# New state of a gated graph layer: turned by VectorE in two pieces instead of by TensorE, with x loaded in short runs and layer 1's rows fetched back from DRAM

## The chip, the cores and the metric

The kernel runs on one core of a Trainium2 chip. The core has TensorE (matmuls, written to PSUM), VectorE (DVE in the profile), ScalarE (ACT), GpSimd (POOL) and SyncE (SP, which here only issues DMAs). GpSimd and SyncE each issue DMAs on a queue of their own, and 16 DMA engines move the data of both. Every engine takes its instructions in the order in which the program gives them. The metric is the device time of one execution in microseconds.

## What is computed

Two residual layers on x (128 graphs, 128 nodes, 256 channels, float32) with an adjacency matrix per graph. Layer 0 normalizes x, applies ReLU, and puts the result h through a convolution branch, a message branch and a gated update; layer 1 works on the first 25 nodes of each graph only.

```python
h = jnp.maximum(_layernorm(x, axis=-1), 0.0)
x = x + _L0_gnn_ref(h, adj, ...)      # layer 0, all 128 nodes
h = jnp.maximum(_layernorm(x, axis=-1), 0.0)
x = x + _L1_gnn_ref(h, adj, ...)      # layer 1: five groups of the first 25 nodes

def _L0_gnn_ref(x, ...):              # x is h here; d = 256
    ...                               # x_conv, x_nmp: the two branches
    x_in = jnp.concatenate([x_conv, x_nmp], axis=-1)
    gi = x_in @ w_ih.T + b_ih
    gh = x @ w_hh.T + b_hh
    ...                               # cut into thirds: r, z, n
    r = jax.nn.sigmoid(gi_r + gh_r)
    z = jax.nn.sigmoid(gi_z + gh_z)
    nn_ = jnp.tanh(gi_n + r * gh_n)
    return (1.0 - z) * nn_ + z * x
```

## The kernel before

The 128 graphs are worked in 32 groups of four (q = 0 to 31). A group's state is kept with channels on the partitions: the tile `hT` is [128 channels, 2 halves of the 256 channels, 512 tokens], the 512 tokens being 4 graphs of 128 nodes. x in DRAM, and the output, have tokens as rows of 256 channels (1 KB), so the new state has to be turned before it is added to x.

There are three stretches. Up to about 690 us the kernel normalizes x, runs the convolution in the frequency domain (`stage_a`, `stage_b`) and, beside it, starts the message branch (`early`). From there to about 1947 us `stage_c(q)` does the gates of one group after the other, with the rest of the message branch and most of layer 1 between its steps. After that only layer 1 is left, which works on blocks of 16 graphs (blocks 0 to 7; block k needs the groups 4k to 4k+3).

The order of all engines' instructions is written by a small planner (`Lane`, `Order`): each piece of work is a generator that yields its cost in TensorE time and a delay before its next step; the planner picks the lane with the least weighted work whose next step is due. A step that waits for a condition polls it every 0.5 us of planned time. So a delay in a `yield` is planned time: it sets where the following instructions stand in each engine's queue, not when they run. Real waits are by semaphore.

One `stage_c(q)`, in the order of its lines:

- L768 to L802: the matmuls of the first gates. ScalarE copies the first product to `u2` (L769); VectorE forms sums of the convolution branch (`tc`, helper at L586). The two early parts (L775) and the three small products (L788, L790) follow, with VectorE's L791 and L792; then L794 with ScalarE's sigmoid into `r`, L797 to L800 with VectorE's L798 (adds a product to `u2`) and L784 (the helper `gate`), then L802.
- L806: the inverse transform of the next group's convolution branch, with block transposes by VectorE (L705, from PSUM).
- L808: wait, in the plan, until group q - 1 has finished its end (`C_DONE`).
- L810 to L831: `z`. L817 and L818 allocate `xt` and load the group's x into it, with four DMAs on SyncE's queue.
- L834 to L862: the candidate state in `r`.
- L863 to L872: for each half of the channels ScalarE takes tanh into `r`, and GpSimd computes (h - n) * z + n with three operations of 128x512: L867, L868, L870. The last writes `z` with its columns permuted. After that the group counts as gated (`G_DONE`), and the next `stage_c` may start.
- L874 to L898, 11 us of planned time later, while the next group is running: TensorE transposes `z` in eight 128x128 pieces (L887) into two PSUM tiles `po`. VectorE adds the x of `xt`: the first 32 nodes of each graph go to the tile `X1` for layer 1 (L890), the other 96 stay in `xt` (L891, L893). GpSimd's queue stores those 96 nodes in four DMAs (L896), whose pieces are single rows of 1 KB. Then `C_DONE`.

Tiles without a `bufs` of their own exist once in this pool: `xt`, `z`, `r` and `u2` among them. `hTc` exists three times, `xm` and `xc` twice. Matmul results of the gates rotate through three PSUM banks (`pgat`), all others through five (`ptmp`).

`rows(q)` waits for `C_DONE` and normalizes the rows of `X1`: VectorE L945 to L947, GpSimd's power (L948), and 4 us of planned time later VectorE L951 and ScalarE L952. `block(blk)` multiplies (L1032, L1049, L1058 ...) and adds the result to `X1` (L1104), which GpSimd's queue stores (L1107). `prepare(blk)` makes layer 1's matrices: GpSimd adds (L970) that VectorE reduces at once (L975), and a chain over L995 to L998.

SyncE's queue carries, in one order, the loads of `hTc` and `xm` (L681, L683, for two groups ahead), of `yt` (L605), of `xt` (L381), of W1 (L935) and of small adjacency pieces (L964).

## Time and profile before

| | |
|---|---|
| median of 3 runs | 2039.76 us (2026.0 to 2566.76) |
| the profiled execution | 2034.12 us |
| its span, first to last instruction | 2032.3 us |
| granted TensorE clock, mean | 0.994 |
| L887, TensorE transposes of z | x256, 273 ns median |
| L890, L891, L893, VectorE adds of x | x32 each, 410, 416 and 681 ns median |
| L705, VectorE block transpose 128x512 from PSUM | x64, 710 ns median |
| L867, L868, L870, GpSimd gate operations 128x512 | x64 each, 1385, 1314 and 1310 ns mean |
| L896, GpSimd's issue of a store of 96 KB | x128, 552 ns median, 3.7 us from issue to landing |
| q0, the DMA queue that GpSimd issues on | 32656 packets, 93.98 MB, 14.2% of 16 engines' span |
| q1, the DMA queue that SyncE issues on | 157062 packets, 185.46 MB, 31.5% |

PE in the profile's lines is TensorE's matmuls, PEld its weight loads, which overlap them. A line of the timeline gives the start in us, the busy time in us, engine, source line, operation, what is written from what, and how many instructions were merged; in brackets stands the idle time of the engine before it and what ended that. A line of the busy times by stretch gives the stretch, its length, then each engine's busy time with its number of instructions, the granted TensorE clock, the DMA engines' busy share and GB/s. In the page's fifth part the groups of instructions carry count, total busy time and mean ns of one.

### The profile page before, as it was taken

Reading aid. Unit: us, or ns where it says so; the run is one execution under the profiler, and the core shown is the slowest. Engines: PE = TensorE matmul, PEld = TensorE weight load, DVE = VectorE, ACT = ScalarE, POOL = GpSimd, SP = SyncE. Lnnn points to the kernel's source line nnn. Section 1 sums busy time; section 2 is a strip of 40 time slices with the busy share of each in tenths; the row PEclk is TensorE's granted clock in tenths of the full one; section 3 lists DMA queues with packets and bytes.
Section 4 is the critical chain, followed back from the end, with each engine's and each line's share of the span. In section 5 each row is a group of like instructions: output and inputs, shape, how many; then the busy total and the mean of one; then the engine's idle time right before and its main releaser. Section 6 shows DMA issues by size and latency. Waiting matters only on the chain.

```text
span 2032.3 us, 34053 instructions
## 1 busy us (share of the span) xinstructions
PE 1989.3 (98%) x12852; PEld 1653.7 (81%) x12852; DVE 1285.2 (63%) x2807; ACT 683.8 (34%) x1547; POOL 741.2 (36%) x898
## 2 busy tenths in 40 slices
PE   7998999999999999999999999999999999999998
PEld 5666888889888888778788878878888888878875
DVE  6774445785433566766775775677577757766643
ACT  4663222454222344232322322232233322232233
POOL 3542666332655022532333233224323323332330
PEclk9999999999999999999999999999999999999999
DMA  9987879744877633432322322322232323232121
GB/s 214 297 266 226 269 255 285 222 145 161 269 257 254 188 115 89 147 90 68 105 73 84 96 83 73 97 83 80 82 108 68 90 84 93 79 100 84 37 82 53
DMA packets 190266, 281.91 MB, mean 139 GB/s; under 512 B 23745, under 2 KB 143494, under 8 KB 190102
## 3 DMA queue, kind: packets, MB, share of 16 engines
q1 hardware_dynamic: 157062, 185.46, 31.5%
q0 software_dynamic: 32656, 93.98, 14.2%
q8 instruction: 102, 1.67, 0.4%
q14 instruction: 62, 0.51, 0.1%
q10 hardware_dynamic: 384, 0.28, 0.1%
HBM read 187.34 MB, written 92.27 MB: 138 GB/s over the span
## 4 chain that ended last, share of the span: by engine, by line
PE 90%; DVE 3%; issue 2%; DMA 2%; POOL 2%; ACT 1%; SPq 0%; POOLq 0%; DVEq 0%; ACTq 0%
PE p L741 41%; PE pa L526 7%; PE pm L630 5%; PE ph L1049 5%; PE pz L1058 5%; PE pc L421 4%; PE pb L526 3%; PE px L656 3%; PE pf L432 3%; PE pi L698 3%; PE po L887 1%; PE ph L410 1%; PE py L1032 1%; PE pw L474 1%; PE pse L614 1%
## 5 line engine op out<-in xcount | busy, mean ns | idle before, releaser
L867 POOL TENSOR_TENSOR hTc<-hTc,r 128x512 f32<-128x512 f32 x64 | 88.7, 1385 | 255.8 <-ACT r L864 255.8
L526 PE MATMUL pa<-wf,X 128*128 128x256 f32 x640 | 152.2, 381 | 0.0
L558 DVE SCALAR_TENSOR_TENSOR y<-pa,kk 128x512 f32<-128x512 f32 x78 | 53.8, 690 | 151.2 <-ACT kk L557 151.1
L896 POOL DMA_DIRECT2D out<-xt x128 | 72.0, 569 | 175.1 <-DVE xt L893 172.0
L741 PE MATMUL p<-th,wrz 128*128 128x256 f32 x512 | 134.6, 385 | 0.0
L741 PE MATMUL p<-tc,wrz 128*128 128x256 f32 x512 | 131.5, 379 | 0.0
L741 PE MATMUL p<-tm,wrz 128*128 128x256 f32 x512 | 131.4, 379 | 0.0
L526 PEld LDWEIGHTS pa<-wf,X 128*128 128x128 f32 x640 | 118.2, 190 | 16.1 <-issue 2.0
L421 PE MATMUL pc<-c1w,hTa 128*128 128x256 f32 x512 | 122.3, 386 | 1.9 <-DVE X L438 1.7
L630 PE MATMUL pm<-wmsg,hT 128*128 128x256 f32 x512 | 123.4, 387 | 0.0
L1051 ACT ACTIVATE hh<-ph,vec 128x96 f32<-128x96 f32 (+3 forms) x160 | 63.8, 401 | 140.8 <-PE ph L1049 131.7
L1049 PE MATMUL ph<-yz,w 128*128 128x96 f32 (+3 forms) x640 | 109.7, 325 | 1.0 <-issue 1.0
L421 PEld LDWEIGHTS pc<-c1w,hTa 128*128 128x128 f32 x512 | 95.0, 192 | 18.9 <-DVE h L424 4.8
L741 PEld LDWEIGHTS p<-th,wrz 128*128 128x128 f32 x512 | 94.6, 190 | 19.1 <-issue 7.4
L630 PEld LDWEIGHTS pm<-wmsg,hT 128*128 128x128 f32 x512 | 97.0, 193 | 16.1 <-issue 1.6
L710 ACT ACTIVATE xc<-xc,t_bn 128x256 f32<-128x256 f32 x128 | 58.0, 500 | 149.2 <-DVE xc L707 149.2
L741 PEld LDWEIGHTS p<-tm,wrz 128*128 128x128 f32 x512 | 97.4, 190 | 13.1
L1058 PE MATMUL pz<-hh,w 128*128 128x96 f32 (+3 forms) x640 | 107.3, 322 | 0.0
L1049 PEld LDWEIGHTS ph<-yz,w 128*128 128x128 f32 x640 | 88.4, 194 | 21.3 <-issue 14.5
L741 PEld LDWEIGHTS p<-tc,wrz 128*128 128x128 f32 x512 | 95.0, 190 | 11.6
L1058 PEld LDWEIGHTS pz<-hh,w 128*128 128x128 f32 x640 | 86.6, 191 | 17.7
L741 PE MATMUL p<-hTc,wrz 128*128 128x256 f32 x384 | 98.9, 380 | 0.0
(200 smaller groups left out, 4579.5 us busy)
## 6 DMA issues: line engine op xcount, KB each, us to landing
wf<-wfd SPq DMA_DIRECT2D x160, 256.0 KB
wfd<-ws POOLq DMA_DIRECT2D x64, 320.0 KB, 9.2
yd<-y POOLq DMA_DIRECT2D x80, 256.0 KB, 4.1
yt<-yd SPq DMA_DIRECT2D x64, 320.0 KB
w<-in_W SPq DMA_DIRECT2D x40, 512.0 KB
xa<-in_x SPq DMA_DIRECT2D x128, 128.0 KB
hTd<-hTa POOLq DMA_DIRECT2D x32, 512.0 KB, 6.5
hT<-hTd SPq DMA_DIRECT2D x32, 512.0 KB
```

The source lines that it names most:

```text
L421: nc.tensor.matmul(pc[:, i], hT[:, k, (2 * h + i) * N:(2 * h + i + 1) * N], c1w[:, k], start=(k == 0), stop=(k == 1))
L432: nc.tensor.matmul(pf[:, i, :F * NB], h1[:, 2 * h + i, k * P:(k + 1) * P], fwd, start=True, stop=True)
L526: nc.tensor.matmul(ps, xk(k), WF[f][:, k, s], start=(k == 0), stop=(k == 1))
L630: nc.tensor.matmul(pm[:, i], hT[:, k, j * N:(j + 1) * N], LATE["wmsg"][:, k], start=(k == 0), stop=(k == 1))
L656: nc.tensor.matmul(px[:, dc, i], msgs[h][:, i, dc * P:(dc + 1) * P], aT[:, 2 * h + i], start=True, stop=True)
L698: nc.tensor.matmul(pi[w * WIDE:(w + 1) * WIDE, :, :, n].rearrange("p k g c -> p g k c"), inv[:F, o:o + WIDE], yt[:, n // 2::2].rearrange(" ...
L741: nc.tensor.matmul(ps[:, m], w[:, i, k, m * P:(m + 1) * P], factor(i, x, t), start=first and j == 0, stop=last and j == len(n) - 1, skip_g ...
L867: nc.gpsimd.tensor_sub(d, d, r[:, dc])
L896: nc.gpsimd.dma_start(out=out[q * GB + j, WIDE:].rearrange("(t n) c -> n t c", n=WIDE), in_=xt[j * WIDE:(j + 1) * WIDE, 1:4])
L1049: nc.tensor.matmul(ph, w1[:, k, m * P:(m + 1) * P], yz[:, k, :, o:o + n], start=(k == 0), stop=(k == 1))
L1051: nc.scalar.activation(hh[:, m], ph, AF.Relu, bias=v("b1", g * 4 + m))
L1058: nc.tensor.matmul(pz, w2[:, g, m, cc * P:(cc + 1) * P], hs[g][:, m], start=(m == 0), stop=(m == 3))
```

## The change

The new state is turned by VectorE, in blocks of 32x32, one half of the channels at a time, inside the following group's `stage_c`; the turned halves are written into `hT`, which is not needed any more. For this x is loaded into `xt` in a matching layout: partition 32a + s holds the tokens 16s to 16s + 15, and of each token the channels 32a to 32a + 31 of both halves. Its pieces in DRAM are 32 channels, 128 bytes. One add of 128x1024 then makes x1 for all 128 nodes. It is stored in the same layout to a DRAM tile `x1d`, and from there SyncE's queue fetches the first 32 nodes into `X1` and moves the other 96 to the output, DRAM to DRAM. Loads of x and stores to `x1d` are issued on GpSimd's queue, four DMAs each with 1024 pieces. The last gate operation writes `z` unpermuted. The plan no longer holds `stage_c(q)` until group q - 1 has finished its end; a lane `fetch` takes over `C_DONE`, 12 us of planned time after the store was issued (6 for the last group), plus 5 us for the fetch.

```diff
@@ pool of DRAM tiles
+    x1d = [dr.tile([GB, N, D], FP, name=f"x1d{q}") for q in range(NQ)]
@@ stage_c
         for operation in todo:
             operation()
         yield 2.6, 0.0
+        turned(q - 1, 1)
         for ps, i in ((p6, 5), (p5, 4)):
             part(ps, wrz, i, early, True, False)
             yield 1.75, 0.0
...
         nc.vector.tensor_tensor(vb, va, h7, ALU.add)
+        turned(q - 1, 0)
         yield 1.3, 0.0
         part(p1, wrz, 1, xs, False, True, True)
...
         gate(r11, h1, 0)
+        returned(q - 1)
         yield 1.3, 0.0
...
-        while q and q - 1 not in C_DONE:
-            yield 0.0, 0.5
         z = fr.tile([P, 2, 512], FP, tag="z", name=f"z{q}")
+        xt = fr.tile([P, 16, 2, WIDE], FP, tag="xt", name=f"xt{q}")
...
-        xt = fr.tile([P, 4, D], FP, tag="xt", name=f"xt{q}")
-        load_x(xt, q)
+        TURN[q] = xt, hT, z
+        for a in range(4):
+            nc.gpsimd.dma_start(out=xt[a * WIDE:(a + 1) * WIDE].rearrange("p b d c -> p (b d) c"),
+                                in_=slices(x[q * GB:(q + 1) * GB])[a])
...
-            pat = "p (j t n) -> p t j n"
-            nc.gpsimd.tensor_add(z[:, dc].rearrange("p (t j n) -> p t j n", t=4, j=GB),
-                                 d.rearrange(pat, j=GB, t=4),
-                                 r[:, dc].rearrange(pat, j=GB, t=4))
+            nc.gpsimd.tensor_add(z[:, dc], d, r[:, dc])
         G_DONE.add(q)
-        yield 0.87, 11.0
+        yield 0.87, 0.0
+        if q == NQ - 1:
+            yield 0.0, 9.0
+            turned(q, 1)
+            turned(q, 0)
+            returned(q)
+
+    def slices(t):
+        return t.rearrange("j n c -> (j n c)").rearrange(
+            "(s k a c) -> a s k c", s=WIDE, k=2 * 16, a=4)
+
+    TURN, T_DONE = {}, set()
+
+    def blocks(hT):
+        return hT.rearrange("p k c -> p (k c)").rearrange("p (b d c) -> p b d c", d=2, c=WIDE)
+
+    def turned(q, dc):
+        if q in TURN:
+            _, hT, z = TURN[q]
+            nc.vector.transpose(blocks(hT)[:, :, dc], z[:, dc].rearrange("p (s b) -> p b s", b=16))
+
+    def returned(q):
+        if q in TURN:
+            xt, hT, _ = TURN.pop(q)
+            xtf = xt.rearrange("p b d c -> p (b d c)")
+            nc.vector.tensor_add(xtf, xtf, blocks(hT).rearrange("p b d c -> p (b d c)"))
+            for a in range(4):
+                nc.gpsimd.dma_start(
+                    out=slices(x1d[q])[a],
+                    in_=xt[a * WIDE:(a + 1) * WIDE].rearrange("p b d c -> p (b d) c"))
+            T_DONE.add(q)
+
+    def fetch(q):
+        while q not in T_DONE:
+            yield 0.0, 0.5
+        yield 0.0, 12.0 if q < NQ - 1 else 6.0
         blk = q // QS
         while blk > 2 and blk - 3 not in F_DONE:
             yield 0.0, 0.5
         if blk not in X1:
-            X1[blk] = fr.tile([P, QS, D], FP, tag="x1", name=f"x1_{blk}", bufs=3)
-        for h in range(2):
-            po = ptmp.tile([P, 2, D], FP, tag="tmp", name=f"po{q}_{h}")
-            for i in range(2):
-                t = 2 * h + i
-                for dc in (1, 0):
-                    nc.tensor.transpose(po[:, i, dc * P:(dc + 1) * P],
-                                        z[:, dc, t * P:(t + 1) * P], ident)
-            if h == 0:
-                nc.vector.tensor_add(X1[blk][:, q % QS], xt[:, 0], po[:, 0])
-                nc.vector.tensor_add(xt[:, 1], xt[:, 1], po[:, 1])
-            else:
-                nc.vector.tensor_add(xt[:, 2:], xt[:, 2:], po)
-        yield 0.9, 1.5
-        for j in range(GB):
-            nc.gpsimd.dma_start(out=out[q * GB + j, WIDE:].rearrange("(t n) c -> n t c", n=WIDE),
-                                in_=xt[j * WIDE:(j + 1) * WIDE, 1:4])
+            X1[blk] = LATE["co"].tile([P, QS, D], FP, tag="x1", name=f"x1_{blk}", bufs=3)
+        nc.sync.dma_start(out=X1[blk][:, q % QS], in_=x1d[q][:, :WIDE])
+        nc.sync.dma_start(out=out[q * GB:(q + 1) * GB, WIDE:], in_=x1d[q][:, WIDE:])
+        yield 0.0, 5.0
         C_DONE.add(q)
@@ the lanes of the last stretch
-    order.run(loads, groups, beside, Lane([rows(q) for q in range(NQ)], ahead=2),
+    order.run(loads, groups, beside, Lane([fetch(q) for q in range(NQ)], ahead=2),
+              Lane([rows(q) for q in range(NQ)], ahead=2),
               Lane(second, ahead=2, weight=0.2))
```

## The prediction

> **What bounds the kernel now.** I read the head and the chain of the page first, then busy times by stretch, then one gated group on each engine.
>
> ```profile
> span 2032.3 us, 34053 instructions
> PE 1989.3 (98%) x12852; PEld 1653.7 (81%) x12852; DVE 1285.2 (63%) x2807; ACT 683.8 (34%) x1547; POOL 741.2 (36%) x898
> ...
> PE 90%; DVE 3%; issue 2%; DMA 2%; POOL 2%; ACT 1%; SPq 0%; POOLq 0%; DVEq 0%; ACTq 0%
> ```
>
> TensorE carries 90% of the chain. The busy times by stretch narrow it to the stage that is changed, 690 to 1947 us:
>
> ```profile
> core 0: us, PE busy (x) PEld busy (x) DVE busy (x) ACT busy (x) POOL busy (x), PEclk, DMA share, GB/s
> 690.00:1947.00 1257.00, 1250.33 (x8161) 1046.68 (x8159) 863.68 (x1803) 380.98 (x823) 399.21 (x451) 1.00 0.30 88
> 1100.00:1947.00 847.00, 847.00 (x5502) 709.82 (x5500) 582.54 (x1216) 247.02 (x538) 273.48 (x304) 1.00 0.28 83
> ```
>
> There TensorE stands still 6.7 us of 1257, and not at all after 1100. A TensorE instruction taken away is time gained, as long as nobody makes TensorE wait. VectorE has a third of its time free, GpSimd two thirds, the DMA engines 70%. The 32 groups come every 39.4 us (first add of L890 at 740.4, last at 1960.4, 31 steps).
>
> I write T for the moment at which a group's last matmul ends. In the group I follow, T is 1405.9 on the timeline. First TensorE's timeline:
>
> ```profile
> 1416.69 0.59 PE L741 MATMUL p<-hTc,wh 128*128 128x256 f32 x2
> 1417.12 1.04 PE L887 MATMUL po<-cst,z 128*128 128x128 f32 x8
> 1417.99 1.03 PE L741 MATMUL p<-tc,wrz 128*128 128x256 f32 x4
> ```
>
> The eight transposes hold TensorE from 1417.12 to 1417.99, 0.87 us. On GpSimd's timeline the six gate operations and the four stores:
>
> ```profile
> 1406.56 1.43 POOL L867 TENSOR_TENSOR hTc<-hTc,r 128x512 f32<-128x512 f32 x1 [1.72 <-ACT r L864]
> ...
> 1413.64 1.27 POOL L870 TENSOR_TENSOR z<-hTc,r 128x512 f32<-128x512 f32 x1
> 1419.53 2.26 POOL L896 DMA_DIRECT2D out<-xt  x4 [4.62 <-DVE xt L893]
> ```
>
> GpSimd finishes half 1 of z at T+4.9 and half 0 at T+9.0. Then VectorE in the same group:
>
> ```profile
> 1409.60 1.49 DVE L586 TENSOR_TENSOR tc<-tc,xc 128x256 f32<-128x256 f32 x1
> 1413.08 0.42 DVE L791 TENSOR_TENSOR ve<-ve,p 128x256 f32<-128x256 f32 x1 [1.99 <-PE p L741]
> 1413.60 0.42 DVE L792 TENSOR_TENSOR ve<-ve,p 128x256 f32<-128x256 f32 x1
> 1416.89 0.69 DVE L798 TENSOR_TENSOR u<-u,p 128x512 f32<-128x512 f32 x1 [2.87 <-PE p L741]
> ```
>
> VectorE is idle T+5.2 to T+7.2 and T+8.1 to T+11.0. The change puts its two transposes into these gaps.
>
> **The change, part by part.**
>
> *Transposes leave TensorE.* 32 groups by 0.87 us = **27.8 us gained**. No other edit touches TensorE.
>
> *VectorE.* Removed per group: 0.41 + 0.42 + 0.68 = 1.51 us (L890, L891, L893). Added: two block transposes of 128x512, 0.71 each by L705 (its source is PSUM and contiguous), and one add of 128x1024. Adds take 0.42 at 256 and 0.69 at 512 columns, so 0.69 + 2 x 0.27 = 1.22. Net 2.64 - 1.51 = +1.13 us. The first transpose stands behind the tc sums, which end at T+5.2, after half 1 is there (T+4.9): no wait. The second stands behind L792 (T+8.1) and waits 0.9 us for half 0; it ends at T+9.7, before L798 has its operand at T+11.0. Queued behind it are L798 and whatever layer 1 has there. The add follows L784 at T+12.0, in the place of the three removed. So the net cost to TensorE is 0.
> The transposes read with a step of 64 bytes beside GpSimd's gate, which no row shows. The tc sums take 1.38 to 1.49 there against 0.42 alone, 3.5 times; so from 0.71 to 0.71 x 3.5 = 2.5 us each. At 2.5 the second ends at T+11.5 and L798 is 0.5 late; the bank it frees is wanted at about T+17. I take 0.71; both ends cost nothing. The contiguous third gate operation is no gain: L870, permuted, takes 1310 ns, L868, plain, 1314.
> The Trainium skill (SBUF — State Buffer, Who interferes with whom) says that a VectorE instruction with two SBUF inputs contends with GpSimd's reads and one with a single SBUF input does not. The tc sums agree with its first half; by its second half the transposes stay at 0.71.
>
> *GpSimd's queue.* Four stores of 96 runs become four of 1024, and four loads of 1024 come from SP's queue. Price of an issue: shortest 0.531 us for 128 runs (L674), 0.578 for 256 (L455), so 0.37 ns a run and 0.578 + 768 x 0.00037 = **0.86 us**. Ends: 0.55 (runs cost nothing, L896) and 5.9 (all of L896's 0.552 is its 96 runs: 0.552 x 1024 / 96). I take 0.86, by the longest list that has a row. Net 8 x 0.86 - 4 x 0.55 = +4.7 us per group of 39.4, of which GpSimd works 12.7.
> The loads of x stand right behind the stores and must wait until these have read xt; GpSimd is held from about T+17 to T+22 and issues until T+25.5. Behind it stand layer 1's small operations: the power of the rows, moved past it to T+33; the eight b additions (L970), for which VectorE's L975 waits, once in four groups; the store of L1107, which nobody awaits. A b addition falls into these 8.5 us in about one group of five, 8 x 0.2 = 1.7 times, at up to 5 us, less 2 that TensorE's banks bear: 5 us; from 0 to 8 x 3 = 24. I take **+4 us**. The gate itself starts 10 us later and is not held.
>
> *DMA engines.* Per group and engine 256 short pieces come in and 256 go out. The trace's packet records have 13 ns for 100 bytes, 19 for 268, 46 for 1024. The line gives **14 ns for 128**, 3.6 us each way. Ends: 5 ns (a packet of 4096 bytes takes 159, and holds 32 pieces) and 92 ns, twice the 1024-byte piece, because no row has a short write to HBM. I take 14, since cost falls with size in all rows. Stores: first issue T+13.4, last at T+16.0, plus L896's 3.7 us to landing and 2 for the shorter pieces: landed at **T+21.7**.
> The Trainium skill (DMA: Bandwidth & Descriptors, Specifications) speaks against this edit: below 512 bytes a DMA engine reads, modifies and writes. Estimated as a doubling to 28 ns, the stores land 3.6 us later and the sum is the same.
>
> *Rows fetched later.* SP waits for that landing, then fetches 128 KB and moves 384 KB DRAM to DRAM. L1107 lands 128 KB of the same shape in 4.3 us; so x1 is there at **T+26**. Behind SP's wait stand the loads of W1 and, a third of a group later, hTc and xm for two groups ahead. The written order lets L945 read x1 17 us after the return at T+10; in the present trace L945 (1425.73) comes 6 us after its planned place (about T+13.4); I take 3 of these 6: T+30. Margin 4 us, so no wait. Layer 1 does not miss the time: block 6's first matmul is at 1942, its last group, 27, ended near 1791.
>
> *The end.* Now the last gate ends at 1955.9, x1h at 1971.5, and block 7 uses it at 1991.1, because TensorE still has block 6. After: two steps on VectorE, GpSimd's queue (busy with L970 until 1960), stores, fetch: x1h some 9 us later, inside the 19. L945 may wait up to 4 us ahead of block 6's copies: **+2 us**.
>
> *Sum* for the profiled execution: span 2032.3 - 27.8 + 4 + 2 = 2010.5, and the 1.8 us around it (2034.12 - 2032.3): **2012 us**. That execution lies 0.3% under the median of 2039.76, whose three runs go from 2026.0 to 2566.76.
>
> **Rivals.**
>
> *Small waits eat it.* VectorE waits in order for GpSimd (the power now falls near the next gate, 8.4 us long, before which or behind which it may be queued) or for x1. For: the order leaves 1 to 4 us in several places. Against: VectorE is idle about a third of each group. At 1 to 2 us per group, 32 to 64 us on 2012: about **2045** to 2076.
>
> *Short pieces are dear* (the other side). x1 then comes after L945, which holds VectorE while TensorE wants its three gate banks emptied; each bank bears a product of 0.87 us, so 1.7 us are free. It decides from the point where the 4 us are used up: 256 d = 26 - 13.7 - 2.5 = 9.8 us, d = 38 ns a piece, or an issue of about 2 us (4 x 1.15 more). At 60 ns: 256 x 22 ns = 5.6 late, 3.9 of it stalls, x 32 = 125: **2137**. At 92 ns: 13.8 late, 12.1 x 32 = 387: 2399. For: no row has short writes. Against: every row with short pieces is cheap, and q0's share is 14.2%.
>
> *Nothing gained*, because the transposes were hidden. That would need TensorE idle beside them; it is not. No separate chance.
>
> *More than 2% gained.* All of TensorE's idle time in the stage and the transposes are 6.7 + 27.8 = 34.5 us, 1.7%: 2000. It takes a lucky pair of runs.
>
> **How the numbers follow.** Forecast (1995 to 2025): 0.51. Small waits within 2%: 0.19, beyond: 0.07. Short pieces dear: 0.18. Over 2% gained: 0.05. Two per cent is about what a measurement of this kernel tells from no change. Faster 0.05; same 0.51 + 0.19 = 0.70; slower 0.07 + 0.18 = 0.25. The range goes from 1992 (34.5 us off the fastest run, 2026.0) to 2100, which leaves out dear pieces (0.18) and no more than 0.02 below.
>
> **What would show it.** Right: L887 gone, TensorE's idle share in the stage as low as now, a GpSimd issue near 0.9 us, short pieces near 14 ns each, L945 without idle time ahead of it. Wrong: VectorE idle ahead of the row statistics, released by a DMA; GpSimd issues of 2 us and more; TensorE waiting for VectorE for more than 2 us per group.

## The result, and the profile after

The changed kernel takes 2045.8 us (median of 8; 2040.3 to 2050.36) against 2035.83 us for the kernel before (median of 8; one of these eight, 2566.76, stands apart and is left out of the ratio). The ratio is **1.0058, 95% interval 1.0044 to 1.0072**: slower by about 12 us (10 by the two medians). The forecast was 2012. 2045.8 is within 2% and inside the stated range, but the sign is the other one: where about 22 us were to be gained, about 12 are lost. The profiled execution took 2045.82 us (before: 2034.12).

The head and the chain on the page of the changed kernel, which answer to the first lines of the prediction:

```profile
span 2043.9 us, 33427 instructions
PE 1975.7 (97%) x12596; PEld 1635.6 (80%) x12596; DVE 1327.4 (65%) x2807; ACT 683.3 (33%) x1547; POOL 865.4 (42%) x1026
...
PE 83%; DVE 5%; DMA 5%; POOL 3%; issue 2%; SPq 1%; ACT 1%; DVEq 0%; POOLq 0%; ACTq 0%
```

TensorE has 256 instructions fewer and is busy 13.6 us less, yet the span is 11.6 us longer. In the chain DVE, DMA and POOL have more weight: 5, 5 and 3%, where they had 3, 2 and 2. The busy times by stretch say where (columns as in the prediction: PE, PEld, DVE, ACT, POOL, then the granted clock):

```profile
1100.00:1947.00 847.00, 842.88 (x5379) 704.01 (x5377) 616.11 (x1228) 248.35 (x544) 362.06 (x396) 0.99 0.40 102
820.00:1100.00 280.00, 261.85 (x1612) 213.53 (x1611) 193.91 (x392) 75.12 (x164) 117.23 (x140) 0.95 0.38 99
1947.00:2043.90 96.90, 81.30 (x530) 59.60 (x526) 33.17 (x87) 30.32 (x70) 21.47 (x30) 0.93 0.27 71
```

The same two last stretches of the kernel before:

```profile
820.00:1100.00 280.00, 274.75 (x1753) 227.03 (x1752) 194.72 (x413) 79.59 (x174) 98.28 (x119) 0.99 0.32 93
1947.00:2032.30 85.30, 77.02 (x512) 56.59 (x510) 27.80 (x77) 28.62 (x66) 19.53 (x28) 0.99 0.25 72
```

From 1100 to 1947 TensorE still hardly stops (4.1 us of 847). The loss sits at the two ends of layer 1's work: in 820 to 1100, where its first blocks begin (18.2 us without work instead of 5.3), and behind the last group (15.6 instead of 8.3). In both the granted clock has fallen too, to 0.95 and 0.93.

**The steady part is as predicted.** The group whose last gate sum (the VectorE add that is L867 in the changed kernel; its start is T here, some 0.2 us behind the end of the last matmul, which is the prediction's T) starts at 1414.2, on VectorE's timeline:

```profile
1414.22 0.42 DVE L867 TENSOR_TENSOR r<-r,p 128x256 f32<-128x256 f32 x1 [0.48 <-PE p L742]
...
1423.06 1.05 DVE L897 STREAM_TRANSPOSE hTc<-z 128x512 f32<-128x512 f32 x1 [2.58 <-POOL z L874]
...
1424.86 1.05 DVE L897 STREAM_TRANSPOSE hTc<-z 128x512 f32<-128x512 f32 x1
...
1426.78 1.22 DVE L904 TENSOR_TENSOR xt<-xt,hTc 128x1024 f32<-128x1024 f32 x1
```

and on GpSimd's:

```profile
1417.59 1.33 POOL L874 TENSOR_TENSOR z<-hTc,r 128x512 f32<-128x512 f32 x1
...
1421.75 1.27 POOL L874 TENSOR_TENSOR z<-hTc,r 128x512 f32<-128x512 f32 x1
1428.30 3.16 POOL L906 DMA_DIRECT2D x1d<-xt  x4 [5.27 <-DVE xt L904]
1436.01 3.14 POOL L822 DMA_DIRECT2D xt<-in_x  x4 [4.55 <-DMA x1d<-xt]
```

The add starts at T+12.6, the stores at T+14.1, they have landed by T+21.2, where SyncE's fetch, which waits for them, is issued, and VectorE reads the rows at T+30.0. The 17 groups from group 10 to group 27 take 645.5 us before (1145.6 to 1791.1) and 628.7 after (1159.2 to 1787.9): **0.99 us gained per group**, for 0.87 predicted.

**Where the time went.** From 690 us on I split the span into three parts: time in which TensorE has no work; half of the time in which the granted clock was 0.5 (the trace records each such period: 3.4, 6.8 or 10.2 us long; the last one ends with the run, is 4.1 us long before and 4.9 after, and is counted whole, though some 2 us of it lie behind the last instruction in both); and the rest, TensorE's work at full clock.

| after 690 us | before | after | difference |
|---|---|---|---|
| TensorE's work at full clock | 1321.9 | 1287.1 | -34.8 |
| no work | 15.0 | 40.5 | +25.5 |
| half of the time at clock 0.5 (10.9 and 52.7 us) | 5.4 | 26.3 | +20.9 |
| sum | 1342.3 | 1353.9 | +11.6 |

The first line holds the transposes and some 4 us of work that fell to the other side of the 690 us mark (over the whole span the same sum gives -31.0); some 2 us of it are not accounted for. The second and third are what the prediction had at +4 and +2. TensorE's waits that are new in the list of waits:

```profile
PE p L742 <- DVE r L862: 11.8, 7, 7.6
PE ph L1075 <- DMA w<-in_W: 9.8, 2, 6.2
...
PE py L1058 <- ACT x1h L978: 4.9, 2, 3.3
```

(us in total, times, longest.) In the kernel before the first had 1.8 us (as L857, 0.8 at most), and neither of the others is in its list at all. The longest one is a chain through three engines; from the timelines of the changed kernel, GpSimd's, VectorE's and TensorE's lines in order of time:

```profile
1019.00 2.93 POOL L996 TENSOR_TENSOR b<-aj,cst 25x400 f32<-25x400 f32 x8 [8.62 <-DMA aj<-in_adj]
1019.98 0.77 DVE L1001 TENSOR_REDUCE dg<-b 25x16 f32<-25x400 f32 x2 [4.79 <-POOL b L996]
1022.13 0.40 DVE L862 TENSOR_TENSOR r<-r,p 128x256 f32<-128x256 f32 x1
1022.59 1.22 PE L742 MATMUL p<-xm,wn 128*128 128x256 f32 x2 [7.61 <-DVE r L862]
```

Layer 1's adjacency pieces (aj) were issued on SyncE at 1006.93, right behind the fetch and the move (1005.67, 1006.26), and came at 1019. GpSimd, VectorE and TensorE each waited in order behind them. The issue is only 3.8 us later than in the kernel before (1003.12); it is the transfer that is slow. By the trace's packet records the 400 packets of 100 bytes of this load went from 1006.31 to 1007.95 before and from 1008.26 to 1018.21 after, while the packets of the move (to 1014.0) and of the load of x in short pieces (to 1017.6) were under way. It is so for each of the blocks 2 to 7: 1.4 to 1.6 us before, 8.2 to 10.8 after. And the clock, by stretches of the same place:

```profile
1017.00:1027.00 10.00, 4.41 (x10) 3.53 (x11) 5.11 (x13) 1.44 (x2) 5.91 (x11) 0.51 0.22 74
1027.00:1034.00 7.00, 5.35 (x28) 4.32 (x27) 5.77 (x6) 1.01 (x2) 5.50 (x5) 0.97 0.00 0
1034.00:1041.00 7.00, 7.00 (x23) 5.87 (x23) 1.48 (x6) 0.74 (x2) 2.07 (x3) 0.52 0.01 2
```

From 1017 the clock is at half, and again from 1034, where TensorE is busy all of 7 us. At the other end of layer 1, SyncE's and TensorE's lines:

```profile
1966.34 0.54 SPq L921 DMA_DIRECT2D x<-x1d  x1
1966.92 0.63 SPq L922 DMA_DIRECT2D out<-x1d  x1
1967.66 0.90 SPq L961 DMA_DIRECT2D w<-in_W  x2
...
1975.55 1.80 PE L1075 MATMUL ph<-yz,w 128*128 128x112 f32 x7 [6.24 <-DMA w<-in_W]
```

SyncE stood at the last group's fetch until its stores had landed; the load of W1 stood behind it, and TensorE waited 6.24 us for that load.

### The profile page after: what moved, and what is told of

The parts are those of the page before. It is cut to its first block, busy times and chain, and to the rows that moved or that the text cites. A ratio compares the mean times of both kernels' runs of the same rounds, so it can differ in the third digit from the quotient of the medians.

```text
span 2043.9 us, 33427 instructions
## 1 busy us (share of the span) xinstructions
PE 1975.7 (97%) x12596; PEld 1635.6 (80%) x12596; DVE 1327.4 (65%) x2807; ACT 683.3 (33%) x1547; POOL 865.4 (42%) x1026
## 3 DMA queue, kind: packets, MB, share of 16 engines
q8 instruction: 100, 1.64, 0.3%
## 4 chain that ended last, share of the span: by engine, by line
PE 83%; DVE 5%; DMA 5%; POOL 3%; issue 2%; SPq 1%; ACT 1%; DVEq 0%; POOLq 0%; ACTq 0%
PE p L742 38%; PE pa L527 7%; PE ph L1075 5%; PE pm L631 5%; PE pz L1084 5%; PE pc L422 4%; PE pb L527 3%; PE pf L433 3%; PE pi L699 3%; PE px L657 3%; PE pw L475 1%; PE ph L411 1%; PE py L1058 1%; DMA x1d<-xt 1%; DMA w<-in_W 1%
## 5 line engine op out<-in xcount | busy, mean ns | idle before, releaser
L906 POOL DMA_DIRECT2D x1d<-xt x128 | 101.3, 818 | 189.0 <-DVE xt L904 183.7
L822 POOL DMA_DIRECT2D xt<-in_x x128 | 100.5, 793 | 132.0 <-DMA x1d<-xt 130.1
L1075 PE MATMUL ph<-yz,w 128*128 128x96 f32 (+3 forms) x640 | 114.1, 335 | 10.8 <-DMA w<-in_W 9.8
L897 DVE STREAM_TRANSPOSE hTc<-z 128x512 f32<-128x512 f32 x64 | 66.8, 1045 | 83.4 <-POOL z L874 83.4
```

What stands on the lines that cost most here:

```text
L822: nc.gpsimd.dma_start(out=xt[a * WIDE:(a + 1) * WIDE].rearrange("p b d c -> p (b d) c"), in_=slices(x[q * GB:(q + 1) * GB])[a])
L897: nc.vector.transpose(blocks(hT)[:, :, dc], z[:, dc].rearrange("p (s b) -> p b s", b=16))
L906: nc.gpsimd.dma_start(out=slices(x1d[q])[a], in_=xt[a * WIDE:(a + 1) * WIDE].rearrange("p b d c -> p (b d) c"))
L1075: nc.tensor.matmul(ph, w1[:, k, m * P:(m + 1) * P], yz[:, k, :, o:o + n], start=(k == 0), stop=(k == 1))
```

## The experiments

Four theories came out of the comparison, and a fifth later. **1**: SyncE stands waiting for the stores to `x1d` (269 us in 58 waits, 27.6 at most), and the loads of W1 and aj behind it come late. (In the kernel before it waits for stores too, ahead of the loads of x: 153.8 us in 53 waits.) **2**: the move DRAM to DRAM fills a few DMA engines with large pieces. In the trace's packet records it goes as 8 packets of 49,152 bytes per group, 1.95 us each at the median, four at a time. The Trainium skill (DMA: Bandwidth & Descriptors, Why a DMA increments its semaphore by 16 and not by 1) has a rule for this: the slowest dimension of both sides decides how many engines share a copy, up to 16; here that dimension is the 4 graphs of the group. The packet records do not name the engine, but they agree: five of these packets are open together for 0.04 us in all, four for 103 us. **3**: VectorE and GpSimd, with their added work and the chain load, GpSimd, VectorE in layer 1's preparation. **4**: layer 1 begins right behind the groups, so rows that come 10 us later stop TensorE. **5**: the end of a group, being inside the following group, comes late where that group is held up.

All runs in one table. Idle and half clock are those of the profiled execution after 690 us, the latter in full length (half of it is lost); that execution can lie up to 7.6 us off the median. The rows come from six sets of runs, each with the kernel before beside it, so they are best compared by their ratios.

| kernel | median us | ratio to before, 95% interval | no work | clock 0.5 |
|---|---|---|---|---|
| changed kernel | 2045.8 | 1.0058 (1.0044 to 1.0072) | 40.5 | 52.7 |
| fetch and move on GpSimd's queue | 2047.15 | 1.0056 (1.0035 to 1.0076) | 38.9 | 43.1 |
| no move | 2034.8 | 0.9992 (0.9977 to 1.0008) | 28.5 | 41.7 |
| move on 16 engines | 2041.15 | 1.0036 (1.0016 to 1.0056) | 36.8 | 51.9 |
| before, without the transposes | 2001.55 | 0.9835 (0.9811 to 0.9859) | 14.5 | 7.3 |
| W1 and aj on ScalarE's queue | 2040.14 | 1.0033 (1.0011 to 1.0054) | 36.6 | 40.3 |
| layer 1 held back | 2037.25 | 1.0028 (1.0006 to 1.0051) | 33.4 | 34.6 |
| these two together | 2057.81 | 1.0125 (1.0093 to 1.0157) | 49.2 | 54.8 |
| fetch and move from x, no wait for the stores | 2031.65 | 0.9996 (0.9975 to 1.0017) | 28.2 | 36.5 |
| preparation relaxed | 2046.19 | 1.0077 (1.0049 to 1.0104) | 42.6 | 55.1 |
| fetch planned 4 us sooner | 2036.36 | 1.0010 (0.9989 to 1.0031) | 35.6 | 36.1 |
| preparation relaxed, W1 and aj on ScalarE | 2050.44 | 1.0086 (1.0054 to 1.0118) | 39.1 | 48.4 |
| all four parts | 2024.16 | 0.9965 (0.9947 to 0.9983) | 27.7 | 28.3 |
| the four without relaxed preparation | 2030.55 | 0.9973 (0.9953 to 0.9993) | 28.8 | 26.4 |
| **the four, last block prepared as it was** | **2024.74** | **0.9940 (0.9918 to 0.9962)** | 24.1 | 29.1 |
| the same, fetch sooner still | 2047.6 | 1.0063 (1.0041 to 1.0086) | 40.8 | 30.0 |
| own end for groups 4, 7, 8 | 2041.38 | 1.0042 (1.0028 to 1.0057) | 37.8 | 43.1 |
| own end for all groups | 2048.03 | 1.0073 (1.0057 to 1.0088) | 46.7 | 35.2 |
| fastest combination, own end for 4, 7, 8 | 2028.77 | 0.9970 (0.9955 to 0.9985) | 27.9 | 27.7 |

### The fetch and the move on GpSimd's queue

```diff
-        nc.sync.dma_start(out=X1[blk][:, q % QS], in_=x1d[q][:, :WIDE])
-        nc.sync.dma_start(out=out[q * GB:(q + 1) * GB, WIDE:], in_=x1d[q][:, WIDE:])
+        nc.gpsimd.dma_start(out=X1[blk][:, q % QS], in_=x1d[q][:, :WIDE])
+        nc.gpsimd.dma_start(out=out[q * GB:(q + 1) * GB, WIDE:], in_=x1d[q][:, WIDE:])
```

> Only edit to the changed kernel: both transfers of the fetch (rows into X1, the other 96 nodes to the output) are issued on GpSimd's queue, behind the loads of x that wait for the same landing anyway. Theory 1 (SyncE stands waiting for the store to x1d, and the loads of W1 and of the adjacency pieces behind it land late): SyncE no longer waits, TensorE's idle time ahead of W1 (9.8 us) and behind the late adjacency (7.6 us) goes with the half clock that follows it, 2012 to 2020 us. Theory 2 (the large pieces of the DRAM to DRAM move fill four of the 16 DMA engines): part of it stays, since the pieces are as large, 2030 to 2040. Theory 3 (neither, VectorE and GpSimd are the cause): 2045 or more, since GpSimd gets two more issues per group.

The time stays (1.0056). TensorE's waits for W1 are gone, and another stands in their place, near the end (1967.52):

```profile
PE pa L1007 <- POOL b L996: 5.5, 1, 5.5
```

The wait for the stores goes with the DMA: what stands behind it on the new queue, layer 1's b additions, is late now. So theory 1 holds for W1, but moving the wait to another queue gains nothing: of the times expected, 2047.15 is theory 3's.

### Without the move, and the move spread

```diff
-        nc.sync.dma_start(out=out[q * GB:(q + 1) * GB, WIDE:], in_=x1d[q][:, WIDE:])
```

> The DRAM to DRAM move of the 96 nodes is left out, so most of the output is not written; the fetch of the rows and SyncE's wait for the store stay. Theory 1: the wait stays, 2035 to 2045. Theory 2: 2012 to 2020. Theory 3: 2045.

```diff
-        nc.sync.dma_start(out=out[q * GB:(q + 1) * GB, WIDE:], in_=x1d[q][:, WIDE:])
+        nc.sync.dma_start(
+            out=out[q * GB:(q + 1) * GB, WIDE:].rearrange("j n c -> n j c"),
+            in_=x1d[q][:, WIDE:].rearrange("j n c -> n j c"))
```

> The move is described with the 96 nodes as its slowest dimension, so that its pieces are rows of 1 KB spread over 16 DMA engines; all else as in the changed kernel. Theory 1: 2040 to 2047. Theory 2: 2015 to 2025. Theory 3: 2045.

Without the move (most of the output is then not written), 0.9992: it costs about 13 us (1.0058 less 0.9992, of 2036). The time is just below theory 1's 2035 to 2045 and far from the 2012 to 2020 of theory 2. The 7.61 us stop shrinks to 3.1, the waits for W1 from 9.8 to 2.6, and the packets of aj ahead of that stop take 4.6 us instead of 9.95. Spread over more engines (its slowest dimension is now 96), 1.0036, theory 1's range: the stop is 6.2, the waits for W1 6.4. So the move costs, and its lying on four engines is the smaller part of that cost, if any: the intervals of the spread move and of the changed kernel, 1.0016 to 1.0056 and 1.0044 to 1.0072, overlap.

### The kernel before, without TensorE's transposes

The adds read `z` in place of the turned tiles, so the new state is added unturned; all else is the kernel before.

> The kernel before, with the eight TensorE transposes of each group left out; VectorE adds the unturned z from SBUF, so the output is not the reference's. It measures the first term of the prediction alone. If TensorE's work is the bound in that stage: 2035 - 28 = 2007 us. If the transposes were hidden: 2030 to 2036.

It gives 0.9835, 33.8 us less than the 2035.37 of its comparison (28 were expected), and the 17 groups take 627.9 us. So the transposes were on TensorE's path in full, and the first term of the sum is right. The work at full clock is 28.8 us less (1293.1 against 1321.9; 27.5 over the whole span). This kernel has almost no half clock after 690, and TensorE stops no longer than before: it is what the change would be if nothing else came with it.

### The loads on ScalarE's queue, layer 1 later, and both

```diff
-            nc.sync.dma_start(out=S["w1", n], in_=W1[n % NG].rearrange("(k p) o -> p k o", p=P))
+            nc.scalar.dma_start(out=S["w1", n], in_=W1[n % NG].rearrange("(k p) o -> p k o", p=P))
...
-            nc.sync.dma_start(out=aj[:, i % 2 * 2 + i // 2::GB],
+            nc.scalar.dma_start(out=aj[:, i % 2 * 2 + i // 2::GB],
```

> The changed kernel with the loads of W1 and of the small adjacency pieces issued on ScalarE's queue instead of SyncE's; TensorE's order is the same. Theory 1 (they stood behind SyncE's wait for the store): the two W1 waits (9.8 us) and the 7.6 us behind the late adjacency go, with the half clock behind them; 2020 to 2028 us, the waits for x1h (4.9 us) stay. Theory 4 (layer 1 starts right behind the groups, so that rows that come later stop TensorE there, whatever the queue): 2035 to 2045, with the loss still between 820 and 1100 us.

The waits for W1 fall from 9.8 to 3.0 us (0.24 at the end in place of 6.24), the ratio to 1.0033. The stop at 1022.7 stays, 8.04 us, and GpSimd still waits for aj (10.43 us). Its packets went from 1012.19 to 1018.41, again until those of the load of x were through (1017.8): its being late is not its place behind SyncE's fetch, but how long the transfer takes beside the change's other transfers. The time is theory 4's (2035 to 2045), not theory 1's.

```diff
-        while len(E_DONE) < NQ:
+        while len(E_DONE) < NQ or 10 not in C_DONE:
```

> The changed kernel with layer 1 held back until group 10's rows are there, so that its blocks run some groups behind; queues as in the changed kernel. Theory 1: the W1 waits stay wherever a store is waited for, 2035 to 2045. Theory 4: the loss between 820 and 1100 us goes (18 us of idle time against 5, and about 9 us of half clock), the end stays: 2020 to 2028.

Layer 1's set-up waits until group 10 has its rows. The stretches show the loss move on:

```profile
820.00:1100.00 280.00, 274.68 (x1802) 234.19 (x1801) 224.14 (x398) 74.73 (x156) 133.06 (x133) 1.00 0.48 123
1100.00:1400.00 300.00, 289.84 (x1800) 233.57 (x1799) 200.30 (x453) 90.79 (x208) 112.68 (x146) 0.98 0.36 94
```

820 to 1100 is healed and 1100 to 1400, whole in the changed kernel, loses 10.2 us. The stage at which layer 1 begins is what loses, not a fixed time. TensorE's waits there are for GpSimd's b additions (6.5 us) and VectorE's sums, and none is for x1h; that speaks for theory 3. Theory 4 had the loss go and the time at 2020 to 2028, and it is 2037.

> Both edits of the two runs before. If the two causes add up, all of the loss but some us at the end goes: 2008 to 2015 us. If one cause was the whole, the time of the better of the two.

Together they take 1.0125, worse than either: the waits for W1 are 11.0 us again (4 times), those for GpSimd's b additions 9.7. These two gains do not add up. Each edit lets the planner write another order, which may be why; that is not shown.

### Fetch and move from x instead of x1d

```diff
-        nc.sync.dma_start(out=X1[blk][:, q % QS], in_=x1d[q][:, :WIDE])
-        nc.sync.dma_start(out=out[q * GB:(q + 1) * GB, WIDE:], in_=x1d[q][:, WIDE:])
+        nc.sync.dma_start(out=X1[blk][:, q % QS], in_=x[q * GB:(q + 1) * GB, :WIDE])
+        nc.sync.dma_start(out=out[q * GB:(q + 1) * GB, WIDE:], in_=x[q * GB:(q + 1) * GB, WIDE:])
```

> The changed kernel, but the two fetches of a group read x itself instead of x1d: same sizes, same queue, same place, but nothing to wait for; layer 1 and the output so miss layer 0's update. Theory 1: SyncE never stands before a store, 2018 to 2026 us. Theory 4: the rows' place in the order is the same and they now come early, so part of the loss between 820 and 1100 us goes too. If the move itself (theory 2) is the cause: 2040 to 2045.

The same bytes move, but SyncE has no store to wait for; layer 0's update is missing from layer 1 and from the output. 0.9996: without SyncE's wait the time is about 12.6 us less. That is rather an upper bound for the wait, since nothing ties the fetch to its group here: that of group 31 is issued 32.6 us ahead of T. No wait for W1 is left, and the time behind the last group is 83.4 us from 1947 instead of 96.9. It lies above the 2018 to 2026 of theory 1 and below the 2040 of the move. What stays is the beginning of layer 1:

```profile
820.00:1100.00 280.00, 264.82 (x1623) 215.91 (x1622) 192.43 (x393) 75.38 (x164) 118.74 (x142) 0.96 0.38 103
```

Some 30 us above the kernel without transposes remain although nobody waits for the stores on SyncE; so theory 1 is less than a third of the 44 us that lie between the changed kernel and that one. The rows of groups 4, 7 and 8 are read at nearly the same places as in the changed kernel (T+64.7, T+38.4 and T+43.3), and TensorE still waits 4.4 us for x1h: what makes these rows late is where the plan puts their reading, not the landing of the stores.

### The preparation relaxed

```diff
-        yield 0.0, 4.0
+        yield 0.0, 14.0
         for r, n, w in _runs():
             nc.gpsimd.tensor_tensor(b1[:, :, r:r + w], aj[:, :, n:n + w],
...
         dg = pool2.tile([NN, SB, NG], FP, tag="dg", name=f"dg{blk}")
+        yield 0.0, 8.0
         for g in range(NG):
             nc.vector.reduce_sum(dg[:, :, g], b1[:, :, OFFS[g]:OFFS[g] + SIZES[g]],
...
-        yield 0.0, 7.0
+        yield 0.0, 4.0
```

> The changed kernel with other planned delays in the preparation of layer 1's blocks alone: 14 us instead of 4 between the loads of the adjacency rows and GpSimd's additions of b, 8 us newly between these and VectorE's reductions, 4 instead of 7 behind them. No instruction is added or left out. Theory 3 (the 7.61 us stop of TensorE at 1022.6 us is the chain load, GpSimd, VectorE, one behind the other in order): the stop goes or falls under 2 us, with the half clock behind it, and the time falls by about 8 to 12 us, to 2030 to 2037. Theory 1 (the standing SyncE alone): the waits for W1 at 1904 and 1976 stay, and the time falls by no more than 4 us. Theory 4 (layer 1 starts too close behind the groups): the later preparation is what the blocks miss next, and the time stays or rises.

The 7.61 us stop goes, as theory 3 has it (0.59 is left at that place), and the time does not fall (1.0077). The list of waits says why:

```profile
PE ph L1076 <- DMA w<-in_W: 12.4, 2, 8.4
...
PE py L1059 <- ACT x1h L978: 8.4, 2, 5.8
```

9.8 has become 12.4, and 4.9 has become 8.4: with the first stop out of the way the rows are the next thing late. This is the outcome expected of theory 4. With the loads on ScalarE's queue besides:

> The delays of the relaxed preparation together with the loads of W1 and of the adjacency rows on ScalarE's queue instead of SyncE's. If the chain of the preparation and the standing SyncE are separate losses, the waits for W1 at 1904 and 1976 go as in the run with these loads on ScalarE (5.7 us), the stop at 1022.6 goes as well, and the time is 2024 to 2031. If the losses are one budget that moves (theory 4), the time stays above 2034.

1.0086, above 2034 by far: taking away both waits gains nothing here, since others come in their place.

### The fetch planned 4 us sooner

```diff
-        yield 0.0, 12.0 if q < NQ - 1 else 6.0
+        yield 0.0, 8.0 if q < NQ - 1 else 6.0
```

> The changed kernel with the planned delay between the last store of a group and the fetch of its rows cut from 12 to 8 us. Theory 4 (the later rows stop TensorE where layer 1 begins): the two waits for x1h (1.65 and 3.27 us at 1032 and 1075) shrink together by 3 us or more, and the time falls by 4 to 7 us, to 2038 to 2042. Theory 1 (SyncE stands waiting for the store): SyncE comes to the fetch 4 us sooner and waits there longer, its waits for x1d rise from 269 us towards 390, and the time stays within 3 us or rises.

1.0010, the best single edit that keeps all work: 9.4 us less than the changed kernel, more than the 4 to 7 expected of theory 4. Both waits for x1h are gone. The time at half clock falls from 52.7 to 36.1 us, which alone is 8.3 us. SyncE does not wait longer:

```profile
SPq L921 <- DMA x1d<-xt: 270.2, 58, 27.9
```

270.2 against 269.4, where theory 1 wanted about 390. In the middle of the program the fetch is still issued at T+21, since the stores land then; what comes sooner is all that stands behind it: the rows are read at T+27.7 instead of T+30.0.

### All four parts

Relaxed preparation, fetch 4 us sooner, loads of W1 and aj on ScalarE's queue, move on 16 engines.

> All at once: the relaxed delays, the fetch 4 us sooner, the loads of W1 and of the adjacency rows on ScalarE's queue, the move of the wide part written so that it is spread over 16 DMA engines. If each of the causes holds its own part, the four add up to 20 to 30 us below the changed kernel: 2015 to 2025, below the kernel before. If the same time only moves from one wait to the next (theory 4), it stays between 2032 and 2042, with new waits between 1100 and 1950.

0.9965: about 19 us below the changed kernel (by the two ratios; 21.6 by the medians), and below the kernel before. The stretch 820 to 1100 is whole again (276.25 of 280). The time is in the range of the first reading (2015 to 2025): together the four parts gain more than any one of them, so the losses are not only one budget that moves from wait to wait. Then the same without the relaxed preparation:

> The run with all four parts, without the relaxed delays of the preparation: what is left is the fetch 4 us sooner, W1 and the adjacency rows on ScalarE's queue, the move on 16 engines. If the relaxed preparation carries a part of that run's gain (it moved the end of group 31 by only 2 us when it stood alone), group 31 ends 5 us or more later than there and the time is 2028 or more. If it cost time instead, by a longer piece behind group 31 (97.4 us there, 84.9 in the kernel before, 107 where the relaxed delays stand alone), that piece falls below 90 us and the time is 2015 to 2021.

0.9973; the last gate sum of group 31 comes 4 us later and the stop is back (6.42 us at 1026). The piece behind it is 92.5 us, so neither half of the expectation came out in full. And with the relaxed preparation for all blocks but the last:

```diff
-        yield 0.0, 14.0
+        yield 0.0, 14.0 if blk < NBLK - 1 else 4.0
...
-        yield 0.0, 8.0
+        yield 0.0, 8.0 if blk < NBLK - 1 else 0.0
...
-        yield 0.0, 4.0
+        yield 0.0, 4.0 if blk < NBLK - 1 else 7.0
```

> All four parts, with the last block's preparation as in the changed kernel and the relaxed delays for the blocks before it. If the piece behind group 31 is long there because the last block's preparation comes late, it falls from 97.4 us to about 86 and the time to 2012 to 2018, the fastest kernel here. If it is long for another reason (the stores and the fetch of the last group), nothing falls and the time stays at 2021 to 2027.

**0.9940 (0.9918 to 0.9962), 2024.74 us**: this version is faster than both kernels, by 0.6% than the kernel before (0.5 by the medians) and, over the two comparisons, by about 1.2% than the changed kernel. From the run with all four parts it is not told apart: the intervals overlap, and so do the times. The time is in the range of the second reading (2021 to 2027), and its piece behind group 31 is still 94.6 us: the last block's preparation was not what lengthened it. Its stretches:

```profile
820.00:1100.00 280.00, 276.34 (x1722) 227.38 (x1721) 201.19 (x417) 81.29 (x178) 124.24 (x147) 0.98 0.46 112
1100.00:1400.00 300.00, 298.96 (x1948) 249.34 (x1948) 218.80 (x446) 90.09 (x194) 132.70 (x141) 1.00 0.44 106
```

Its fetch planned 4 us sooner once more (8 to 4; 6 to 4 for the last group):

> As the run with the last block's preparation as it was, with the planned delay ahead of the fetch cut once more, from 8 to 4 us (from 6 to 4 for the last group). If late rows still cost time at layer 1's start, another 3 to 8 us go. If 8 us was enough and the wait on SyncE for the stores now stands in the way (its waits for x1d grow beyond 300 us), the time stays or rises by up to 5 us.

1.0063: 23 us lost, where a rise of up to 5 was expected, without a longer wait on SyncE (289 us against 292). From 1100 to 1950 TensorE loses 4 to 10 us in each of three stretches, through many waits of up to 4 us. A fetch that is planned sooner only helped once; why 4 us is so much worse than 8 is open, beyond the fact that another order was written.

### The end of a group outside the following group

The add L904 starts at T+11 to T+17 as a rule, but at T+45.9, T+21.5 and T+23.2 for groups 4, 7 and 8, and their rows are read at T+64.6, T+40.0 and T+43.4 (before: T+33.1, T+21.5, T+19.6). These are the groups where layer 1 begins. Theory 5 puts that down to the change's place for the end of a group.

```diff
+    def own_end(q):
+        return q in (4, 7, 8, NQ - 1)
...
-        turned(q - 1, 1)
+        if not own_end(q - 1):
+            turned(q - 1, 1)
...
-        if q == NQ - 1:
+        if own_end(q):
             yield 0.0, 9.0
             turned(q, 1)
             turned(q, 0)
             returned(q)
```

> In the changed kernel the add L904 of a group starts 12.6 us behind its last gate sum as a rule, but 45.9, 21.5 and 23.2 us behind it for groups 4, 7 and 8, whose following stage_c is held up by layer 1's first blocks; in the kernel before the end of a group had a delay of its own and stood behind no such steps. This run gives groups 4, 7 and 8 an end of their own again (transposes and add 9 us of planned time behind the gates, beside the following stage_c, as for the last group), the others stay. Theory 5 (the rows come late at layer 1's start because a group's end is bound to the steps of the following group): the adds of 4, 7 and 8 come within 16 us, the waits of TensorE for x1h (4.9 us) go, and the time falls by 5 us or more, to 2036 to 2041. If the rows are late by the stores and the fetch alone, the x1h waits stay above 3 us and the time within 3 us.

The adds come at T+41.0, T+17.9 and T+15.5, the rows still at T+60.7, T+38.3 and T+43.1, and the waits for x1h stay (4.6 us). The time is 1.0042, 4.4 us under the changed kernel's median, with intervals that overlap. For groups 7 and 8 theory 5 falls as the cause of the late rows: their adds are 3.6 and 7.6 us earlier and their rows are not, or by less than 2 us. For group 4, whose add still comes at T+41.0, this run does not test it.

> The same for all 32 groups: nothing of a group's end stands inside the following group. Theory 5: as with groups 4, 7 and 8 alone, since the others are on time in either place: 2036 to 2043. If the place between given steps also kept VectorE's queue free of waits for the gates, TensorE now waits for VectorE's sums in many groups and the time is 2050 or more.

For all groups, 1.0073 (2048.03, 2 us short of the 2050 of the other reading). The 17 groups from 10 to 27 take 645.3 us, the time of the kernel before: the whole gain per group is gone. In these groups TensorE is 12.2 us without work, 11.1 of it through one line of the waits, which has 15.5 us from 690 on:

```profile
PE p L742 <- DVE z L819: 15.5, 23, 1.4
```

So the place of the two transposes between given steps of the following group is worth as much as taking them from TensorE. In the fastest combination:

> The fastest combination so far (rows 4 us sooner, loads of W1 and of the adjacency rows on ScalarE's queue, move on 16 engines, relaxed preparation except for the last block), with an end of their own for groups 4, 7 and 8. In that combination TensorE does not wait for x1h any more, so by theory 5 little is left to gain: 2018 to 2026. If the late adds still cost through what stands behind them (the loads of x, the next fetch), it falls below 2018.

0.9970 (2028.77, above the 2018 to 2026 expected) for 0.9940 without it: nothing is left to gain there.

## Why the prediction was wrong

**"Transposes leave TensorE": right.** The kernel before without its transposes has 28.8 us less work at full clock, for the 27.8 predicted; the steady groups of the changed kernel gain 0.99 us each, for 0.87.

**"VectorE", net cost 0: right, with a wait that was not seen.** A transpose takes 1.05 us, not 0.71 (inside 0.71 to 2.5), and GpSimd is not the reason: the three of the 64 that ran beside one of its operations took 1.04 to 1.05 us like the others. The add takes 1.22, as computed. But "no wait" is wrong: VectorE waits 83.4 us in 32 groups for L874, 2.6 each. The first transpose could start only at 1423.06, when the second half of z was done (1423.02), not the first (1418.9). By the code, each transpose writes 32-column blocks all over `hT`, and GpSimd's operations of the other half still read their part of `hT` until then. It cost TensorE nothing in the steady part (300.00 us busy of 300 from 1100 to 1400), as long as it stands where it was put (the run with an own end for all groups).

**"GpSimd's queue": issue and hold right, "+4 us" mis-sized (its own product, 1.7 by 3, is 5).** The issue measured 0.79 and 0.81 us at the median for 0.86; GpSimd is held to T+24.9 for T+25.5. The b additions did hold VectorE and TensorE, once, for 7.61 us with 10.2 us at half clock, some 13 us in all. What they waited for in that case was the load of aj, whose transfer took 9.95 us for 1.64, not GpSimd's hold.

**"DMA engines": right for the short pieces, silent on what stands beside them.** A packet of 4,096 bytes of the stores, 32 pieces of 128 bytes, takes 308 ns at the median, about 10 ns a piece (14 taken, 5 to 92 as bounds); one of the loads of x takes about 235, some 7 a piece. The stores landed at T+21.2 for T+21.7. The rival *Short pieces are dear* is out, and the doubling to 28 ns does not show. What the term left out is the load of aj in the same stretch: in the blocks 2 to 7 its packets need 8.2 to 10.8 us instead of 1.4 to 1.6. Without the move it is still 4.6 to 7.2 us, so the move is a part of it; the rest was not separated.

**"Rows fetched later": the step that failed.** Its times hold in the steady part to within half a microsecond (T+21.2 and T+30.0). It failed in three ways. First, it named the loads of W1 as standing behind SyncE's wait and gave that no price. The runs showed 9.8 us of TensorE waiting for W1, and up to about 12.6 us of the time for SyncE's wait in all (the run that fetches from x). Second, "Layer 1 does not miss the time" was read at block 6, where rows lie 150 us ahead. At the other end they do not: row 7 was read at 1046.0 and used at 1051.9 in the kernel before, and is read at 1064.7 after, where TensorE then stands 3.27 us for it. A margin read at one block was taken for all. Third, the move was named with its 384 KB and given no price; leaving it out gives about 13 us. These 13 and the 12.6 overlap (both take away most of the waiting for W1) and are not to be summed. The lines for row 7, of the kernel before on VectorE and TensorE, then of the changed one:

```profile
1045.99 0.42 DVE L945 BATCH_NORM_STATS2 st<-x 128x6 f32<-128x256 f32 x1
1051.91 0.88 PE L1032 MATMUL py<-r,x1h 128*128 128x212 f32 x4
...
1064.66 0.42 DVE L971 BATCH_NORM_STATS2 st<-x 128x6 f32<-128x256 f32 x1
1074.58 1.24 PE L1058 MATMUL py<-r,x1h 128*128 128x212 f32 x4 [3.27 <-ACT x1h L978]
```

**"The end", +2 us: mis-sized.** From the last gate sum to the end it took 84.9 us before and 97.8 after: +12.9, of which 6.24 is the wait for W1 and 5.1 the half clock beside it (10.2 us from 1969.5).

**No term at all: the clock.** 20.9 us, nearly three quarters of the 28.8 gained, went to half clock. That is how 25.5 us more of waits came to cost 46. Three of the ten periods of half clock after 690 us have no stop beside them, so not all of the 20.9 can be laid to the waits.

The rival *Small waits eat it*, 2045 to 2076, has the time right and the place wrong: it wanted 1 to 2 us in every group, and the steady groups lose nothing. The waits are few, large and at layer 1's beginning and end.

What stays open: why the preparation of layer 1's first blocks and their rows compete so that taking away one wait makes the next (the relaxed preparation, the two together), and why the fetch 8 us sooner loses what 4 us gained. Every edit of a delay changes the written order on all engines, so these runs are not clean tests of one wait. The part of the 13 us of the move that is its place on the queue, and the part that is its bytes, was not separated. Between the fastest version and the kernel before without transposes some 21 us remain (0.9940 and 0.9835; 25 in the profiled executions): more waits (24.1 us for 14.5), more half clock (29.1 for 7.3) and some 5 us of work at full clock, whose causes stay open.

## What to carry to other kernels

A TensorE instruction taken out of a full TensorE is worth its time, but price the start and the end of the pipeline too: read the slack of a moved result at its first use, not in the steady part. When a DMA with a wait goes onto a queue, list what stands behind it and when each item is needed; moving the wait to another queue only changed who was late here. Price what new DMA traffic does to the small loads beside it, not only its own time. Add to the new stops of TensorE what half clock may take beside them: here nearly as much again.

## What the runs showed of the hardware

- **Half clock beside short stops.** In the changed kernel each of the six stops of 1.65 us or more after 690 us (1.65, 2.53, 3.27, 3.52, 6.24, 7.61) has a period of clock 0.5 beside it, of 3.4 us, or 6.8 to 10.2 by the longest ones and the one that follows closely. Three such periods (863, 1263 and 1864) have no stop beside them, and in other runs stops of this size have no such period: 2.36 us at 893 with the fetch 4 us sooner, 3.23 us at 1147 with layer 1 held back. The Trainium skill (TensorE: Matmul & The Clock Gate, Part 1: The HAM clock gate) gives an idle window of about 3.4 us as the condition for half rate; the lengths agree with that window, the stops of 1.65 to 3.3 us are shorter than it, so here half clock came without a whole idle window. What else brings it is open.
- **A copy of [4][24576] elements DRAM to DRAM** went as packets of 49,152 bytes and 1.95 us, four at a time; written with 96 as its slowest dimension it went in packets of 1,024 bytes. What that gained (ratio 1.0036 for 1.0058) is not told from nothing: the intervals overlap.
- **A small load beside other transfers can take six times as long.** The 400 packets of 100 bytes of one block's adjacency took 1.4 to 1.6 us in the kernel before and 8.2 to 10.8 in the changed one (blocks 2 to 7), beside loads in 128-byte pieces and the copy of 49,152-byte packets; 4.6 to 7.2 without that copy.
- **The price of issuing on GpSimd's queue** grows slowly with the runs: 0.53 us for 128, 0.58 for 256, 0.79 to 0.81 for 1024.
- **A block transpose of 128x512 in SBUF with a read step of 64 bytes** took 1.05 us, contiguous from PSUM 0.71. Source and step both differ, and the runs do not separate them.
